# Four reorderings in a fused attention and feed-forward block: sums, norms, a copy and three tiles' products change places

## The chip, the cores and the metric

The kernel runs on one core of a Trainium2 chip. A core has a matmul engine (TensorE, PE in the profile; PEld is its weight load), a vector engine (VectorE, DVE), an activation engine (ScalarE, ACT), a general engine (GpSimd, POOL) and SyncE (SP), which here only issues DMAs. Each engine takes its own instructions in the order in which the program wrote them, and waits on semaphores for the others. The metric is the time of one execution on the device in microseconds (us); lower is better.

## The reference

Eight sequences of 1024 rows and 256 columns pass through an attention without learned projections and then through a feed-forward block. Both are wrapped in a layer norm whose scale, shift and gate come from a small vector per sequence:

```python
h = _layernorm(x, axis=-1) * (1 + ca) + sa
x = x + ga * _L0_attn_ref(h, L0_attn_w_lhs, L0_attn_w_rhs)
h = _layernorm(x, axis=-1) * (1 + cb) + sb
x = x + gb * _L0_ffn_ref(h, L0_ffn_W1, L0_ffn_b1, L0_ffn_W2, L0_ffn_b2)
```

The attention is `softmax((h * w_lhs) @ (h * w_rhs).T) @ h`, and the feed-forward block is `relu(h @ W1 + b1) @ W2 + b2` with 1024 inner columns. All is float32.

## The kernel before

**Tiles and stages.** A sequence is a "batch" b (0 to 7) of eight row tiles i of 128 rows; a half g is four of them. The main loop runs over (b, i). In iteration (b, i) the kernel works on several things at once: it makes the scores of the tile two ahead (`direct`, L410, copied out of PSUM by ACT, L417), mirrors them into the rows below, since scores of a symmetric kind are computed once (`mirror`: a DVE transpose L433, four DMA writes and one read through DRAM by SP), takes the row maximum of that tile (`row_max`, L460), turns the maximum into a row with a PE transpose (`max_turn`, L465), subtracts it (`subtract`, L472) and takes the exponential (`exponent`, L481); multiplies the weights with the values (`product`, L493, or the pair functions at L544 and L584 that save products by sums); and does one piece of the feed-forward of the batch before. The tiles with i % 4 below 2 are called "first" in the code and carry the feed-forward's first layer; the other two carry its second layer (`y_first`, `y_second`, L798).

**Order.** The order of the instructions is written out by hand. Each call in the loop emits its instructions to the queues of its engines at that point, and a pinning step keeps that order on each engine. So to move a call is to move its instructions on each engine that it uses, and on no other. Small sums for POOL are kept in a list (`later`), of which `spare()` emits one at a time.

**The first layer.** It is done in chunks c of pairs of inner column blocks. `pair_products(b, g, c)` emits the products pa, pb and pc (L718) and an ACT copy of pa, called kept (L739). `pair_sums` emits four DVE sums (L754, L757, L760, L763) that read pb, pc and kept; when it is done the PSUM banks of pb and pc are free again. `pair_last` emits one more product into pa, a DVE sum (L771) and a POOL sum (L772). `pair_relu` emits two ACT relus (L781, L782) on the tile f, and `pair_turn` four POOL sums (L791 to L794). In the last batch pb lies in another group of PSUM banks.

**Norms.** `ffn_rstd` emits two ACT operations, a logarithm and an exponential (L245, L246), that make one over the root of a variance; the variance is made by `pair_stats` (DVE, L239 and L240). `ffn_norm` makes the normalised rows X, in batch 0, half 0, with four DVE operations (L655), elsewhere with ACT (L650). In iteration (0, 6) `norms` calls just that `ffn_norm(0, 0)`; `ffn_blocks(0, 0)` returns at once. In (0, 7), `ffn_turn(0, 0)` transposes these rows on PE (L687) and shifts and scales them into hT on DVE and ACT (L697, L699); POOL then makes the sums hs (L706 to L709).

**The last phase.** After the loop the feed-forward of the last batch is done with W2 multiplied by the gate (w2g). For each half g it does four chunks of the first layer, and then `second(b, a, parts, cut)` for the four tiles a: eight products (L903) over the inner column blocks, in the order 0, 4, 1, 5, 2, 6, 3, 7. Part 0 is the first `cut` of them (here six), part 1 the rest; the last two need the relu of the last chunk. `second_out` adds the rows x on DVE (L917) and has SP write them out (L919, L921), tiles in pairs, but for the last two.

Of the kernel before, what the change touches and what calls it, by code (L numbers as in the profile page):

```python
# [24 lines left out]
def adaln_block_kernel(  # L25
# [14 lines left out]
    B, S, D = x.shape  # L40
# [3 lines left out]
    NI = INTER // P  # L44
    HALF = 512
    TH = HALF // P
# [411 lines left out]
    def row_max(b, i):  # L458
        m = work.tile([P, 1], F32, tag="m", name=f"m_{b}_{i}")
        nc.vector.tensor_reduce(m, score_row(b, i), AX.XY, ALU.max)  # L460
        max_t[b, i] = m
# [167 lines left out]
    def spare():  # L629
        if queue:  # L630
            queue.popleft()()
# [4 lines left out]
    def ffn_rstd(b, g):  # L636
        mv = mvb_t.pop((b, g))
        ffn["r", g] = mv, rstd_of(mv, "rb", f"rb_{b}_{g}")
# [140 lines left out]
    def pair_relu(c):  # L779
        f = ffn["f"]  # L780
        nc.scalar.activation(f[:, c, :], f[:, c, :], AF.Relu)  # L781
        nc.scalar.activation(f[:, c + NH, :], f[:, c + NH, :], AF.Relu)  # L782
# [325 lines left out]
    def norms(b, i):  # L1108
        if b > 0 and i == 0:
            ffn_blocks(b - 1, 1)  # L1110
        if b == 0:
            if i == 0:
                prepare_start(1)
                prepare_stats(1, 0)
            elif i == 1:
                prepare_stats(1, 1)
                sum_w1()
        elif b + 1 < B:
            if i == 1:
                prepare_start(b + 1)  # L1120
                prepare_stats(b + 1, 0)
            elif i == 2:
                prepare_blocks(b + 1, 0)
                x_plus(b + 1, 0)
                xg_times(b + 1, 0)
        elif i == 4:

            ffn_blocks(b, 0)
        if b == B - 1:
            return  # L1130
        if i == 6:
            if b == 0:
                ffn_norm(b, 0)
            ffn_blocks(b, 0)
# [7 lines left out]
    for b in range(B):  # L1142
        for i in range(NT):
# [8 lines left out]
            if (b, i) == (0, NT - 2):  # L1152

                prepare_turn(1, 1)
                product(b, i)
                direct(*ahead)
                exponent(*last_exponent)
                product_out(b, i)
                mirror(*ahead)
                early(b, i)  # L1160
                for _ in range(4):
                    spare()
                row_max(*ahead)
                late, last_exponent = ahead, None
                norms(b, i)
                continue
            if ahead and ahead != (0, 2):
                direct(*ahead)
# [34 lines left out]
            if first:  # L1203

                ub, ug = (b - 1, 0) if i >= TH else (b - 2, 1)
                back = i % TH == 0 and ub >= 0
                pair_products(fb, fg, c, turn_max)
                if i == 0:
                    ffn_rstd(b - 1, 1)
                if (b, i) == (1, 0):  # L1210
                    weights(*late)
                    late = None
                if i == TH + 1:
                    pair_relu(c - 1)
                pair_sums(fb, fg, c)
                if ahead:
                    mirror(*ahead)
                pair_last(fb, fg, c)
                if (b, i) == (B - 1, TH):
                    pair_stats(b, 2)  # L1220
                    ffn_rstd(b, 0)
                if i == 0 and back:
                    for q in range(2):
                        y_add(ub, ug, q)
                if i == TH + 1:
                    pair_turn(c - 1)
                if i == 4 and b + 1 < B:
                    prepare_blocks(b + 1, 1)
                    xg_times(b + 1, 1)
                if late:  # L1230
                    subtract(*late)
                pair_products(fb, fg, c + 1, (lambda: max_turn(*extra)) if extra else None)
                if i == 5:
                    exponent(*late)
                    if b + 1 < B:
                        prepare_turn_apart(b + 1, 1, 1)
                        prepare_turn_apart(b + 1, 1, 0)
                pair_relu(c)
                sides_too = i == 4 and b + 1 < B
                if sides_too:  # L1240
                    prepare_turn_apart(b + 1, 0, 1)
                if late and i != 5:
                    exponent(*late)
                if sides_too:
                    prepare_turn_apart(b + 1, 0, 0)
                middle(b, i)
                pair_sums(fb, fg, c + 1)
                pair_last(fb, fg, c + 1)
                if ahead and ahead != extra:
                    row_max(*ahead)  # L1250
                pair_turn(c)
                if i == 0:
                    right_sums(b, (3,))
                    pair_relu(c + 1)
                    pair_turn(c + 1)
                elif back:
                    for q in range(2):
                        y_add(ub, ug, q)
                if c > 0:
                    pair_relu(c + 1)  # L1260
                    pair_turn(c + 1)
            else:
                half = i % TH - 2
                if i == 3 and b + 1 < B:
                    prepare_stats(b + 1, 1)
                if half == 0:
                    if i == 2:
                        pair_begin(b, i, turn_max)
                    else:
                        pair_begin(b, i, lambda: (max_turn(*late), weights(*late)))  # L1270
                elif not ahead:

                    pair_end(b, i - 1)
                    pair_out(b, i - 1)
                    pair_stats(b, i - 1)
                if half:
                    y_second(fb, fg, turn_max)
                else:
                    y_first(fb, fg)
                if i == NT - 2 and (b, 2) in two_t:  # L1280
                    pair_stats(b, 2)
                if ahead:
                    mirror(*ahead)
                if i == 2 and b + 1 < B:
                    prepare_rstd(b + 1, 0)
                elif i == 3 and b + 1 < B:
                    prepare_rstd(b + 1, 1)
                elif i == 6 and b + 1 < B:
                    ffn_rstd(b, 0)
                elif i == NT - 1 and b == B - 1:  # L1290
                    ffn_rstd(b, 1)
                if half == 0:
                    pair_begin_sum(b, i)
                    if i == 2:
                        weights(*late)
                    left_sums(b, i)
                spare()
                early(b, i)
                if late and half:
                    weights(*late)  # L1300
                middle(b, i)
                if i == 2 and b + 1 < B:
                    load_x(b + 1, 1)
                if i == 3 and b + 1 < B:
                    prepare_norm(b + 1, 1)
                    x_plus(b + 1, 1)
                spare()
                if ahead:
                    row_max(*ahead)
                if half:  # L1310
                    y_second_sums(fb)
                else:
                    y_first_sums()
                spare()
# [32 lines left out]
    b = B - 1  # L1347
    for g in range(NT // TH):
        for c in range(NH):
            pair_products(b, g, c)  # L1350
            if g == 0 and c == 0:
                ffn_norm(b, 1)
                ffn_bias(b, 1)
            spare()
            spare()
            if c > 1:
                pair_relu(c - 2)
            if c > 0:
                pair_last(b, g, c - 1)
            pair_sums(b, g, c)  # L1360
            if g == 0 and c == 1:
                ffn_blocks(b, 1)
            elif g == 0 and c == 2:
                y_turn(b - 1, 1)
        pair_relu(NH - 2)
        pair_last(b, g, NH - 1)
        pair_relu(NH - 1)
        if g == 0:
            y_add(b - 1, 1, 0)
            y_add(b - 1, 1, 1)  # L1370
            y_out(b - 1, 1)
            ffn_turn(b, 1)
        for a in range(g * TH, (g + 1) * TH, 2):

            second(b, a, (0,), NI - 2)
            second(b, a + 1, (0,), NI - 2)
            second(b, a, (1,), NI - 2)
            second_out(b, a)
            second(b, a + 1, (1,), NI - 2)
            second_out(b, a + 1)  # L1380
            for _ in range(4):
                spare()
    pin(pin_from)


# [37 lines left out]
```

## Time and profile before

| | |
|---|---|
| Runs (three) | 769.8, 769.78 and 769.23 us; median 769.78 us |
| The profiled execution | 769.46 us, of which the span of the profile is 767.7 us |
| PE busy | 756.5 us, 99% of the span, 3708 matmuls |
| DVE busy | 566.0 us, 74% |
| POOL busy | 538.9 us, 70% |
| ACT busy | 375.0 us, 49% |
| DMA | 95.18 MB moved, mean 124 GB/s |
| TensorE clock granted | 0.9 or more in each of 40 slices |

How to read it: a busy share is an average over all stages. PE's end times are modelled and neighbouring matmuls overlap in the record, so the start of the next matmul tells more than the end of the last one. "Idle before, releaser" names the instruction that ended an engine's idle time. Idle time of an engine other than the one that sets the pace costs nothing by itself. The span runs from the first to the last instruction of the program; the execution's time includes 1.76 us around it.

### The profile page before, as it was taken

The numbers are of one execution on the slowest core, as the hardware profiler recorded it, in microseconds if no ns is written. First come the engines' busy times: TensorE is split into PE (matmuls) and PEld (weight loads), VectorE is DVE, ScalarE is ACT, GpSimd is POOL, SyncE is SP. The second block draws the span as 40 slices with busy tenths as digits, with TensorE's granted clock in tenths as the row PEclk, the third lists the DMA queues.
The fourth block names the chain that finished last, engine by engine and source line by source line (L and its number), as shares of the span: only waits on it lengthen the run. The fifth ranks groups of instructions, "written<-read, shape, count | busy, mean of one in ns | idle before, by whom it ended". The sixth has DMA issues, their size and how long they took to land.

```text
span 767.7 us, 11489 instructions
## 1 busy us (share of the span) xinstructions
PE 756.5 (99%) x3708; PEld 621.7 (81%) x3708; DVE 566.0 (74%) x1222; ACT 375.0 (49%) x681; POOL 538.9 (70%) x632
## 2 busy tenths in 40 slices
PE   8999999999999999999999999999999999999998
PEld 3576789888887888878888888988888788879886
DVE  6697779678796787858787787966879677594632
ACT  4464545635465355555546444563546535252511
POOL 4643975978859697587868787597884979469641
PEclk9999999999999999999999999999999999999999
DMA  5314434365343553535443554436534354142220
GB/s 194 124 50 137 116 104 109 112 192 168 93 131 107 183 150 111 151 102 160 139 124 122 151 151 131 107 117 189 163 98 131 104 159 139 33 134 80 82 83 27
DMA packets 106211, 95.18 MB, mean 124 GB/s; under 512 B 29700, under 2 KB 98848, under 8 KB 106152
## 3 DMA queue, kind: packets, MB, share of 16 engines
q1 hardware_dynamic: 98408, 85.81, 38.1%
q10 hardware_dynamic: 7744, 8.65, 3.7%
q8 instruction: 29, 0.48, 0.2%
q14 instruction: 30, 0.25, 0.1%
HBM read 50.62 MB, written 43.81 MB: 123 GB/s over the span
## 4 chain that ended last, share of the span: by engine, by line
PE 93%; DVE 3%; POOL 1%; issue 1%; ACT 1%; DMA 1%; SPq 0%; DVEq 0%; POOLq 0%
PE po L493 16%; PE psc L410 15%; PE pa L718 10%; PE pb L718 7%; PE pc L718 7%; PE yc L798 6%; PE ya L798 6%; PE yb L798 6%; PE pr L584 5%; PE pq L584 3%; PE pp L544 3%; PE py L903 3%; PE yd L798 3%; PE pm L465 1%; POOL xg L285 1%
## 5 line engine op out<-in xcount | busy, mean ns | idle before, releaser
L772 POOL TENSOR_TENSOR f<-f,kept 128x512 f32<-128x512 f32 x64 | 81.5, 1273 | 105.6 <-DVE f L771 100.2
L410 PE MATMUL psc<-rT,lT 128*128 128x512 f32 (+3 forms) x384 | 134.6, 486 | 0.0
L493 PE MATMUL po<-xg,pT 128*128 128x257 f32 x576 | 131.6, 380 | 0.0
L493 PEld LDWEIGHTS po<-xg,pT 128*128 128x128 f32 x576 | 108.8, 190 | 16.0 <-issue 1.0
L472 DVE TENSOR_TENSOR pT<-sc,pm 128x1024 f32<-128x1024 f32 x64 | 77.1, 1205 | 29.0 <-PE pm L465 24.9
L410 PEld LDWEIGHTS psc<-rT,lT 128*128 128x128 f32 x384 | 67.6, 190 | 38.0 <-issue 26.3
L417 ACT COPY sc<-psc 128x512 f32<-128x512 f32 (+3 forms) x96 | 44.9, 476 | 108.3 <-PE psc L410 94.7
L481 ACT ACTIVATE pT<-pT 128x1024 f32<-128x1024 f32 x64 | 67.4, 1052 | 34.6 <-DVE pT L472 34.6
L460 DVE TENSOR_REDUCE m<-sc 128x1 f32<-128x1024 f32 x64 | 77.3, 1208 | 0.0
L739 ACT COPY kept<-pa 128x512 f32<-128x512 f32 x64 | 37.3, 583 | 79.6 <-PE pa L718 79.6
L718 PE MATMUL pb<-hs,w1s 128*128 128x256 f32 x256 | 65.8, 379 | 1.0 <-DVE f L757 1.0
L718 PE MATMUL pc<-hT,w 128*128 128x256 f32 x256 | 65.7, 379 | 0.0
L781 ACT ACTIVATE f<-f 128x512 f32<-128x512 f32 x64 | 40.1, 626 | 48.6 <-POOL f L772 48.4
L634 POOL TENSOR_TENSOR x<-x,rows 128x256 f32<-128x256 f32 x64 | 45.3, 741 | 22.3 <-DVE x L509 11.8
L718 PEld LDWEIGHTS pb<-hs,w1s 128*128 128x128 f32 x256 | 48.0, 190 | 8.5 <-DVE f L757 1.4
L718 PEld LDWEIGHTS pc<-hT,w 128*128 128x128 f32 x256 | 48.6, 190 | 6.6
L798 PE MATMUL yc<-f,w2s 128*128 128x256 f32 x224 | 52.1, 379 | 0.0
L798 PEld LDWEIGHTS yc<-f,w2s 128*128 128x128 f32 x224 | 41.5, 190 | 10.1 <-issue 2.9
L433 DVE STREAM_TRANSPOSE Tm<-sc 128x896 f32<-128x896 f32 (+6 forms) x49 | 34.7, 707 | 13.3 <-ACT sc L417 12.6
L793 POOL TENSOR_TENSOR ft<-ft,f 128x256 f32<-128x256 f32 x56 | 40.8, 728 | 4.4
L792 POOL TENSOR_TENSOR ft<-ft,f 128x256 f32<-128x256 f32 x56 | 40.8, 728 | 4.4
L791 POOL TENSOR_TENSOR ft<-f 128x256 f32<-128x256 f32 x56 | 40.9, 731 | 3.4 <-ACT f L782 3.4
(165 smaller groups left out, 1670.2 us busy)
## 6 DMA issues: line engine op xcount, KB each, us to landing
D_f<-T_f SPq DMA_DIRECT2D x60, 128.0 KB, 2.7
X_f<-D_f SPq DMA_DIRECT2D x15, 512.0 KB, 3.8
D_a<-T_a SPq DMA_DIRECT2D x56, 128.0 KB, 3.2
D_y<-T_y SPq DMA_DIRECT2D x56, 128.0 KB, 3.0
Y<-D_y SPq DMA_DIRECT2D x14, 512.0 KB, 3.3
out_dram<-x SPq DMA_DIRECT2D x14, 512.0 KB, 3.9
X_a<-D_a SPq DMA_DIRECT2D x13, 512.0 KB, 3.6
x<-in_L_attn_x_dram ACTq DMA_DIRECT2D x12, 512.0 KB, 4.1
```

The costliest lines, as they stand in the source:

```text
L410: nc.tensor.matmul(psc[:, : hi - lo], lhsT=lT_t[b, i // TH][:, k, ts(i % TH, P)], rhs=rT_t[b, n][:, k, lo - n * HALF : HALF], start=(k == ...
L417: nc.scalar.copy(score_row(b, i)[:, lo // V : hi // V, :], psc[:, : hi - lo].rearrange("p (n v) -> p n v", v=V),)
L460: nc.vector.tensor_reduce(m, score_row(b, i), AX.XY, ALU.max)
L472: nc.vector.tensor_tensor(pT.rearrange("p j (a v) -> p j a v", v=V), score_columns(b, i), pm[:, :P].rearrange("p (j a v) -> p j a v", j=1, ...
L481: nc.scalar.activation(pT_t[b, i], pT_t[b, i], AF.Exp)
L493: nc.tensor.matmul(po[:, : D + 1], lhsT=pT[:, t, :], rhs=xg_t[b][:, t, 0 : D + 1], start=(t == 0), stop=(t == NT - 1),)
L584: nc.tensor.matmul(out, lhsT=lhs[:, t, :], rhs=rhs[:, t, :], start=(t == 0), stop=(t == TH - 1),)
L634: queue.append(lambda: nc.gpsimd.tensor_tensor(out, in0, row, op))
L718: nc.tensor.matmul(out, lhsT=lhsT, rhs=rhs, start=True, stop=True)
L772: nc.gpsimd.tensor_tensor(f[:, c::NH, hi], f[:, c::NH, hi], kept[:, None, hi].to_broadcast([P, 2, H2]), ALU.add,)
L791: add(ft[:, 0, c], f[:, c + NH, hi], f[:, c, hi], ALU.subtract)
L798: nc.tensor.matmul(out, lhsT=lhs(c), rhs=rhs(c), start=(c == 0), stop=(c == NH - 1))
```

## The change

Four calls, or groups of calls, change places; nothing is added or taken away.

1. In iteration (0, 6) `norms(b, i)` (four DVE operations) is emitted before `row_max(*ahead)` (one), not after it.
2. In iteration (1, 0) `weights(*late)`, which is the subtraction on DVE and the exponential on ACT for tile (1, 0), is emitted after `pair_sums` of the first chunk and not before it. The lines with `TH + 1` move in the text only; they belong to other iterations.
3. In iteration (7, 4) `ffn_rstd(b, 0)` is emitted after the products of the second chunk, and so after that chunk's copy kept on ACT.
4. In the last phase the first six products of three tiles of a half are emitted one tile after another. Then the last two products and the output of each of the three follow, and then all eight products and the output of the fourth tile. Before, two tiles' first parts came together, then their last parts, and then the next two tiles.

```diff
@@ -1160,9 +1160,9 @@
                 early(b, i)
                 for _ in range(4):
                     spare()
+                norms(b, i)
                 row_max(*ahead)
                 late, last_exponent = ahead, None
-                norms(b, i)
                 continue
@@ -1207,18 +1207,17 @@
                 pair_products(fb, fg, c, turn_max)
                 if i == 0:
                     ffn_rstd(b - 1, 1)
+                if i == TH + 1:
+                    pair_relu(c - 1)
+                pair_sums(fb, fg, c)
                 if (b, i) == (1, 0):
                     weights(*late)
                     late = None
-                if i == TH + 1:
-                    pair_relu(c - 1)
-                pair_sums(fb, fg, c)
                 if ahead:
                     mirror(*ahead)
                 pair_last(fb, fg, c)
                 if (b, i) == (B - 1, TH):
                     pair_stats(b, 2)
-                    ffn_rstd(b, 0)
@@ -1230,6 +1229,8 @@
                 if late:
                     subtract(*late)
                 pair_products(fb, fg, c + 1, (lambda: max_turn(*extra)) if extra else None)
+                if (b, i) == (B - 1, TH):
+                    ffn_rstd(b, 0)
                 if i == 5:
@@ -1370,16 +1371,15 @@
-        for a in range(g * TH, (g + 1) * TH, 2):
-
+        tiles = range(g * TH, (g + 1) * TH)
+
+        for a in tiles[:3]:
             second(b, a, (0,), NI - 2)
-            second(b, a + 1, (0,), NI - 2)
-            second(b, a, (1,), NI - 2)
+        for a in tiles:
+            second(b, a, (0, 1) if a == tiles[3] else (1,), NI - 2)
             second_out(b, a)
-            second(b, a + 1, (1,), NI - 2)
-            second_out(b, a + 1)
-            for _ in range(4):
-                spare()
+            spare()
+            spare()
```

Names used below: TH is 4 (tiles in a half), NI is 8 (inner column blocks), B is 8.

## The prediction

> **What bounds the kernel now.** I read the page first, then the waits of TensorE (PE) alone, then the timeline around each wait and around the end. All times are in microseconds (us) from the start of the span.
>
> ```profile
> PE 93%; DVE 3%; POOL 1%; issue 1%; ACT 1%; DMA 1%; SPq 0%; DVEq 0%; POOLq 0%
> ```
>
> This is the head of the chain that ended last: 93% of it is matmuls. PE is the bound, and a change pays only where PE stands still. The waits of PE, with total, number and longest, name four places that the change touches:
>
> ```profile
> PE pa L718 <- ACT kept L739: 1.4, 1, 1.4
> PE py L903 <- ACT f L781: 1.1, 2, 0.7
> PE pb L718 <- DVE f L757: 1.0, 1, 1.0
> ...
> PE ptx L687 <- DVE X_f L655: 0.2, 1, 0.2
> ```
>
> Modelled ends blur these figures, so I measure each wait by start to start. The timeline (start, length, engine, line, operation, tiles, count, and the idle time before it) shows where they stand, first on PE:
>
> ```profile
> 71.24 1.74 PE L687 MATMUL ptx<-ident,X_f 128*128 128x128 f32 x8 [0.24 <-DVE X_f L655]
> ...
> 82.43 0.59 PE L718 MATMUL pa<-hs,w 128*128 128x256 f32 x2
> 84.02 1.13 PE L718 MATMUL pb<-hs,w1s 128*128 128x256 f32 x4 [1.00 <-DVE f L757]
> ...
> 677.98 0.70 PE L718 MATMUL pa<-hT,w1s 128*128 128x256 f32 x2 [1.36 <-ACT kept L739]
> ...
> 702.64 1.95 PE L584 MATMUL pq<-tsum,pT 128*128 128x129 f32 x16
> ...
> 722.59 1.89 PE L903 MATMUL py<-w2g,f 128*128 128x256 f32 x8
> 725.17 12.50 PE L903 MATMUL py<-w2g,f 128*128 128x256 f32 x56 [0.69 <-ACT f L781]
> ```
>
> and then what stands in front of it on the other engines:
>
> ```profile
> 69.68 1.18 DVE L460 TENSOR_REDUCE m<-sc 128x1 f32<-128x1024 f32 x1
> 70.78 1.37 DVE L655 TENSOR_SCALAR X_f<-x,mvb,rb 128x256 f32<-128x256 f32 x4
> ...
> 81.76 1.22 DVE L472 TENSOR_TENSOR pT<-sc,pm 128x1024 f32<-128x1024 f32 x1 [2.74 <-PE pm L465]
> ...
> 676.92 0.30 ACT L245 ACTIVATE rb<-mvb,eps 128x4 f32<-128x4 f32 x1 [4.48 <-DVE mvb L240]
> ...
> 700.97 1.27 POOL L566 TENSOR_TENSOR pT<-s,pT 128x512 f32<-128x512 f32 x1
> ```
>
> A maximum stands before the norms at 69.68, a subtraction before the sums at 81.76, a root before a copy (677.36 to 677.93) at 676.92; and in the last phase PE stops after 8 matmuls, which are four products, as each product of 256 columns is issued as two.
>
> **What the Trainium skill says.** "Perfetto Trace Analysis", section "Tensor Engine Instruction (MATMUL, LD_WEIGHTS)", has ACT, DVE and GpSimd as strict FIFO and the matmul end as estimated. The trace agrees: the copy at 677.36 has its input from the matmul that starts at 674.30, and still follows the root. "SBUF — State Buffer", section "SBUF: two separate sides", names a port lock between a DVE operation with two SBUF inputs and a GpSimd operation. All sums and subtractions moved here read one operand from PSUM, so I charge nothing; the trace has POOL's L529 at 1.27 beside the subtraction's 1.22, both as elsewhere. "DMA: Bandwidth & Descriptors", section "Anatomy of one DMA — SWDGE (gpsimd) path", puts most of a fixed 2 us of a transfer into the write receipt. Here the last 128 KB write, issued by SP's queue, lands 1.7 after its issue; I use that.
>
> **Part A: norms before the maximum, iteration (0,6).** Nothing is added. The four norms (L655, 1.37) change places with one row maximum (1.18 of L460, 1.10 start to start). The norms start at 69.68 and end at 71.05, and the maximum ends at the old 72.15. The last score matmul starts at 70.41 and keeps PE for 0.43, so PE could transpose from 70.84. In place of eight transposes paced by the norms, it does eight at 0.107, ending at 71.70 instead of 72.81: -1.11. The maximum is read by the transpose at 81.45 and has nine microseconds of slack. The mirror transpose (72.07) and hT (72.96) come after both and do not move. So POOL's row hs, w2s, tsum, which starts at 73.81 and runs without a gap to 85.66, doesn't move either; hs ends at 76.70, and PE reads it at 78.86 - 1.11 = 77.75.
>
> **Part B: sums before the subtraction, iteration (1,0).** The matmul pb of the second pair waits for a PSUM bank that L757 of the first pair frees at 83.97, because L754 and L757 stand behind the subtraction (1.22). Unstalled, pb would start at 82.86 and its second matmul at 83.07 instead of 84.34: 1.26. With A, the first pair's pb ends at 79.64. Then L754 starts at 79.74, L757 at 80.26, L760 at 80.66, L763 ends at 81.47, and the subtraction runs from 81.39 to 82.60. Behind the subtraction on DVE stand the mirror of row 2 and L771, all still earlier than before. Behind it through the data stands the exponential on ACT (82.64 to 83.69), and behind that on ACT the copy kept of the second pair, to 84.17. This is the wait that replaces the old one: PE reaches the last product of the second pair at 85.96 - 1.11 - 1.26 = 83.59 and starts it at 84.22. Measured starts after a stall (84.02, then 84.34) cost a further 0.10. The gain after that is 1.64 and not 2.37.
>
> A second limit follows. POOL is busy to 85.66, so L772 gains only 0.27, and with it on ACT the relus, the norms L650, the exponential and the copy at 93.09, all in a row: that copy now ends near 93.2. PE would read it at 94.73 - 1.64 = 93.09. About 0.2 goes with restart: A and B together give 1.45. Bounds: 1.2 if POOL and ACT run a little later, 1.7 if the copy is in time. DVE and POOL catch up at their next idle times (1.83 at 99.92 and 0.80 at 105.76), and from there on everything hangs on PE, batch after batch (143.93, 235.04, 326.15 for the same row, 91.11 apart), so the gain should last.
>
> **Part C: the copy before the root, iteration (7,4).** The copy's input ends near 674.9, the root's at 676.89. With the copy first, PE goes on at 676.46 instead of 677.98, with 0.10 of restart less: -1.6 at that place. But DVE's row does not move: it is without idle time from 670.07 to 681.17. So L771 ends at 680.05 as before, and POOL starts L772 at 680.19, and from there POOL has no gap until L567 ends at 703.65. At the end of that row PE needs L566 (ends 702.24) for pq at 702.64: slack 0.40. PE arrives 1.5 early, waits for L564, L565 and L566 in turn, and starts pq at 702.30 with a restart of 0.10. Kept: 0.24. Bounds: 0 if the restarts cost more, 1.6 if POOL's row shifts after all. The root itself still waits for L240 at 676.89, so nothing behind it on ACT is later. L320 may come 0.5 earlier, without a reader in need.
>
> **Part D: three tiles' early products first, last batch.** Per half the same 32 products run, the first six of the first tile in the old order. PE waits at the fifth product, for the relu that ends at 725.12, and this wait stays: 0.86 start to start here, 0.59 in the second half (751.92). What the change covers better is the relu of the last pair; it ends at 727.60, and PE came to it after 12 products, at 725.17 + 8 x 0.43 = 728.6, so it waited for nothing. Gain 0. The adds L917 of the first tiles and the write of tiles 4 and 5 come some 2.4 later (757.95 to about 760.3), tile 6 earlier, tile 7 not at all, and tile 7's write at 764.86, landed at 766.57, sets the end. POOL's list of spare work is empty by then (last L634 at 718.05). SP's order of writes is unchanged. Bounds: -0.2 to +0.2.
>
> **The sum.** 1.45 + 0.24 + 0 = 1.69. The profiled execution took 769.46, with 1.76 around its span of 767.7; less 1.69 that is 767.77. It lies 0.32 under the median of the runs shown, 769.78, from which the sum gives 768.09. I forecast 767.9, between the two. A measurement of this kernel can tell about 0.2% (1.54) from no change, and the forecast lies close to that line.
>
> **Rivals.**
> 1. *More is given back* (17%): POOL's fixed row in batch 1 holds PE longer than 0.2, as L772 (85.89, 0.23 after L529) and the relus behind it hardly move. For: POOL idles only 0.23, 0.77 and 0.40 up to 96.82. Against: 1.83 at 99.92. With 0.8 from A and B and 0.2 from C: 768.6.
> 2. *C keeps its full wait* (13%): POOL's row is not the limit, for example because the norms' earlier end pulls it forward. For: 1.36 is the largest single wait. Against: POOL shows no idle from 680.19 on. 1.45 + 1.5 = 2.95: 766.7.
> 3. *The waits only change their names* (5%): the reordering doesn't reach what it aims at, as I expect of D, and A and B are lost in batch 1 too: 769.6.
> 4. *Slower* (7%): the place is the ACT queue in (1,0). The subtraction now waits for all four sums, and each microsecond that it comes later delays the exponential, the copy behind it and PE's last product. The old start of that product, 85.96, is reached if the subtraction starts at 83.1; with C's 0.24 counted, the kernel is slower by 1.5 if it starts past 84.9, and then stands at 771.2. That takes a sum held by 3.5 more than computed, which no row shows.
>
> **How the numbers follow.** The main case has 58%, from 767.2 to 768.5. Range: from 766.5 (rival 2) to 769.0 (most of rival 1); left out are slower, unchanged and a few per cent at the ends. Faster by over 0.2% means below 768.24: four fifths of the main case and all of rival 2, 60%. Slower by over 0.2% is rival 4, 7%. The rest, 33%, lies within 0.2%.
>
> **What would show it.** A: the transposes ptx start at 0.11 apart near 70.85, with po near 71.7. B: no wait of pb for L757, a short new one for kept L739 near 84, another near 93. C: no wait near 678, three short waits of PE for POOL near 698 to 701 in L584. D: the two waits of py for L781 remain. The prediction fails if PE waits at other places in batches 1 to 6, if pq has no wait at all, or if py's waits shrink.

## The result and the profile after

| | before | after |
|---|---|---|
| Median of 19 runs each | 769.73 us | 768.27 us |
| Range of these runs | 769.23 to 771.0 us | 767.67 to 769.02 us |
| Ratio of after to before, 95% interval | | 0.998 (0.9973 to 0.9987) |
| Span of the profiled execution | 767.7 us | 766.5 us |

The kernel became 1.46 us (0.19%) faster at the median, and the interval leaves out no change. The median lies 0.37 us over the forecast of 767.9. It also lies 0.03 us over 768.24, the prediction's line for "faster by over 0.2%", and so in the band to which it gave 33% and not in the one to which it gave 60%.

The head of the chain that ended last, on the page of the kernel after:

```profile
PE 95%; DVE 2%; POOL 1%; DMA 1%; issue 1%; ACT 1%; SPq 0%; POOLq 0%; DVEq 0%
```

and the waits of PE in it (total, times, longest, in us):

```profile
PE py L903 <- ACT f L781: 1.1, 2, 0.7
...
PE pa L718 <- ACT kept L739: 0.5, 1, 0.5
...
PE pq L584 <- POOL pT L566: 0.3, 1, 0.3
PE pr L584 <- POOL pT L565: 0.2, 1, 0.2
```

Three old waits are gone from this list: ptx for DVE, pb for L757, and the 1.4 of pa for kept in the last batch. In their places stand three new, shorter ones, and py's wait stands there untouched. (A fourth that is new, 0.6 of pth at 10.59, belongs to the start of the program, which differs from run to run.) The timeline of PE after, at these places:

```profile
71.18 1.04 PE L687 MATMUL ptx<-ident,X_f 128*128 128x128 f32 x8
...
82.10 1.03 PE L718 MATMUL pb<-hs,w1s 128*128 128x256 f32 x4
...
84.64 0.70 PE L718 MATMUL pa<-hT,w1s 128*128 128x256 f32 x2 [0.54 <-ACT kept L739]
...
675.40 0.59 PE L718 MATMUL pa<-hT,w1s 128*128 128x256 f32 x2
...
698.58 1.16 PE L584 MATMUL pr<-tsum,s 128*128 128x128 f32 x8
699.93 1.16 PE L584 MATMUL pr<-tsum,pT 128*128 128x128 f32 x8 [0.19 <-POOL pT L565]
701.34 2.05 PE L584 MATMUL pq<-tsum,pT 128*128 128x129 f32 x16 [0.25 <-POOL pT L566]
...
721.39 1.89 PE L903 MATMUL py<-w2g,f 128*128 128x256 f32 x8
723.97 12.50 PE L903 MATMUL py<-w2g,f 128*128 128x256 f32 x56 [0.69 <-ACT f L781]
```

The eight transposes now take 1.04 and not 1.74. pb follows its predecessor without a wait, and 2.5 us later pa waits for the copy. In the last batch pa starts with no wait at 675.40, and PE then stands three times in L584: 0.25, 0.46 and 0.52 by the starts against before, of which the view marks only the last two.

To follow a gain through the program, I take the start of the same matmul in two traces; a negative shift means earlier. The first 70 us differ from run to run (the last score matmul ahead of the transposes ptx lay between 0.15 us earlier and 0.51 later than before in the traces of this study), so each row is counted from that matmul. Here po is the product of the attention in that iteration, and "after pb" and "behind pq" mean from the second matmul of each on:

| Start of PE's work, against before | at po (0,7) | after pb (1,0) | at po (1,0) | in (1,1) to (7,4) | at po (7,4) | behind pq (7,7) | at the end |
|---|---|---|---|---|---|---|---|
| after | -1.10 | -2.37 | -1.57 | -1.41 | -3.03 | -1.55 | -1.54 |

That one row is the whole story: 2.37 is gained, 0.80 and then 0.16 are given back; 1.62 is gained, 1.48 is given back; the last phase adds nothing.

### The profile page after: what moved, and what is told of

Read it like the earlier page. It is cut to its first block, busy times and chain, and to the rows that moved or that the text cites. A ratio compares the mean times of both kernels' runs of the same rounds, so it can differ in the third digit from the quotient of the medians.

```text
span 766.5 us, 11489 instructions
## 1 busy us (share of the span) xinstructions
PE 756.5 (99%) x3708; PEld 621.8 (81%) x3708; DVE 566.4 (74%) x1222; ACT 374.9 (49%) x681; POOL 539.3 (70%) x632
## 4 chain that ended last, share of the span: by engine, by line
PE 95%; DVE 2%; POOL 1%; DMA 1%; issue 1%; ACT 1%; SPq 0%; POOLq 0%; DVEq 0%
PE po L493 16%; PE psc L410 16%; PE pa L718 10%; PE pb L718 7%; PE pc L718 7%; PE yc L798 6%; PE ya L798 6%; PE yb L798 6%; PE pr L584 5%; PE pq L584 3%; PE pp L544 3%; PE py L903 3%; PE yd L798 3%; PE pm L465 1%; POOL xg L285 1%; DMA x<-in_L_attn_x_dram 1%
## 5 line engine op out<-in xcount | busy, mean ns | idle before, releaser
L772 POOL TENSOR_TENSOR f<-f,kept 128x512 f32<-128x512 f32 x64 | 81.5, 1275 | 101.9 <-DVE f L771 96.8
L718 PE MATMUL pb<-hs,w1s 128*128 128x256 f32 x256 | 65.8, 379 | 0.0
L718 PE MATMUL pc<-hT,w 128*128 128x256 f32 x256 | 65.7, 379 | 0.0
L781 ACT ACTIVATE f<-f 128x512 f32<-128x512 f32 x64 | 40.1, 626 | 50.2 <-POOL f L772 50.1
L634 POOL TENSOR_TENSOR x<-x,rows 128x256 f32<-128x256 f32 x64 | 45.4, 743 | 22.3 <-DVE x L509 11.8
L718 PEld LDWEIGHTS pb<-hs,w1s 128*128 128x128 f32 x256 | 48.1, 190 | 7.5 <-DVE f L757 0.4
L718 PEld LDWEIGHTS pc<-hT,w 128*128 128x128 f32 x256 | 48.6, 190 | 6.6
L798 PE MATMUL yc<-f,w2s 128*128 128x256 f32 x224 | 52.1, 379 | 0.0
L798 PEld LDWEIGHTS yc<-f,w2s 128*128 128x128 f32 x224 | 41.5, 190 | 10.1 <-issue 2.9
L791 POOL TENSOR_TENSOR ft<-f 128x256 f32<-128x256 f32 x56 | 41.0, 732 | 4.5 <-ACT f L782 4.4
L792 POOL TENSOR_TENSOR ft<-ft,f 128x256 f32<-128x256 f32 x56 | 40.8, 729 | 4.4
```

Of the source, the lines that this page charges most:

```text
L634: queue.append(lambda: nc.gpsimd.tensor_tensor(out, in0, row, op))
L718: nc.tensor.matmul(out, lhsT=lhsT, rhs=rhs, start=True, stop=True)
L772: nc.gpsimd.tensor_tensor(f[:, c::NH, hi], f[:, c::NH, hi], kept[:, None, hi].to_broadcast([P, 2, H2]), ALU.add,)
L791: add(ft[:, 0, c], f[:, c + NH, hi], f[:, c, hi], ALU.subtract)
L798: nc.tensor.matmul(out, lhsT=lhs(c), rhs=rhs(c), start=(c == 0), stop=(c == NH - 1))
```

## The experiments

The ratios are to runs of the kernel before that were taken beside each group, with medians of 769.63 to 769.66 us. "Shift" is the start of PE's last work against before, counted as above, from one trace of each kernel.

| Run | Median us | Ratio to before (95%) | Shift |
|---|---|---|---|
| e1_norms: A alone | 768.53 | 0.9985 (0.9979 to 0.9992) | -1.10 |
| e2_sums: B alone | 769.13 | 0.9993 (0.9985 to 1.0001) | -0.47 |
| e3_root: C alone | 769.57 | 0.9998 (0.999 to 1.0006) | -0.20 |
| e4_tiles: D alone | 769.62 | 1.0001 (0.9993 to 1.0009) | -0.01 |
| e5_exp: after, later exponential | 767.94 | 0.9977 (0.9968 to 0.9986) | -1.55 |
| e6_tsum: that, tsum moved | 767.54 | 0.9971 (0.9959 to 0.9983) | -2.20 |
| e7_yadd: after, y_add on DVE | 767.06 | 0.9965 (0.9953 to 0.9978) | -2.55 |
| e8_cut: after, cut of four | 766.14 | 0.9952 (0.994 to 0.9965) | -3.51 |
| e10_cutpair: before, cut of four | 768.43 | 0.9987 (0.998 to 0.9993) | -1.31 |
| e9_all: after, all of these | 764.88 | 0.9939 (0.9927 to 0.9952) | -5.07 |

### The four parts, each alone

A alone (e1_norms):

```diff
+                norms(b, i)
                 row_max(*ahead)
                 late, last_exponent = ahead, None
-                norms(b, i)
```

> Part A alone on the kernel before (norms ahead of the maximum in iteration (0,6)). Theory: the eight transposes ptx run 0.11 us apart, po starts 1.1 us sooner after the last score matmul, and all of it lasts to the end, because the limits behind it (the kept copy of (1,1) near 93.2) leave 1.5 us of room: -1.1 us, ratio 0.9986. Rival (POOL's fixed row in batch 1 gives more back): the trace shows a new wait of PE between 73 and 105, and at most -0.6 us is left.

Measured: 768.53 us, shift -1.10 at po, and -1.10 to -1.11 at every place behind it. PE's timeline in this run:

```profile
70.69 1.04 PE L687 MATMUL ptx<-ident,X_f 128*128 128x128 f32 x8
71.56 3.63 PE L493 MATMUL po<-xg,pT 128*128 128x257 f32 x16
```

From the first transpose to po it is 0.87 us, where the working had 0.86 (eight times 0.107). The rival that POOL's row takes part of A alone falls.

B alone (e2_sums):

```diff
+                pair_sums(fb, fg, c)
                 if (b, i) == (1, 0):
                     weights(*late)
                     late = None
-                pair_sums(fb, fg, c)
```

> Part B alone on the kernel before (four sums ahead of the subtraction in (1,0)). Theory: the wait of pb for L757 (1.26 us start to start) goes, the copy kept of the second pair stands behind a later exponential and holds PE's last product of that pair for about 0.6 us: -0.55 us is left, ratio 0.9993. Rival 1 (the exponential is no limit): -1.26 us and no wait for kept. Rival 2 (the later subtraction costs more than the wait): no change or slower.

Measured: 769.13 us. The shift is -1.27 behind pb and -0.47 behind the new wait, which is this one (in order of time: the exponential on ACT, the copy behind it, and PE, which waits for the copy):

```profile
83.96 1.06 ACT L481 ACTIVATE pT<-pT 128x1024 f32<-128x1024 f32 x1 [2.87 <-DVE pT L472]
...
84.92 0.57 ACT L739 COPY kept<-pa 128x512 f32<-128x512 f32 x1
...
85.54 0.70 PE L718 MATMUL pa<-hT,w1s 128*128 128x256 f32 x2 [0.54 <-ACT kept L739]
```

The copy's input is ready at 83.2 (the end of the matmul that starts at 82.57), and the copy runs at 84.92, behind the exponential. So 0.80 of the 1.27 is a wait with a new name. Both rivals fall by the trace; the interval of the times alone still holds no change.

C alone (e3_root):

```diff
                     pair_stats(b, 2)
-                    ffn_rstd(b, 0)
...
                 pair_products(fb, fg, c + 1, (lambda: max_turn(*extra)) if extra else None)
+                if (b, i) == (B - 1, TH):
+                    ffn_rstd(b, 0)
```

> Part C alone on the kernel before (copy ahead of the root in (7,4)). Theory: PE starts the product behind the copy 1.5 us sooner, and then waits two or three times for POOL's sums L564 to L566 in (7,7): -0.15 to -0.25 us is left, ratio 0.9997. Rival (POOL's row moves with PE): -1.5 us, no wait in L584.

Measured: 769.57 us; the interval of the times alone can't tell it from no change. The trace can: the shift is -1.64 at po of (7,4), -1.37 a few microseconds on, and -0.19 behind pq, where PE stands just as in the kernel after:

```profile
699.89 1.16 PE L584 MATMUL pr<-tsum,s 128*128 128x128 f32 x8
701.24 1.16 PE L584 MATMUL pr<-tsum,pT 128*128 128x128 f32 x8 [0.19 <-POOL pT L565]
702.65 2.05 PE L584 MATMUL pq<-tsum,pT 128*128 128x129 f32 x16 [0.25 <-POOL pT L566]
```

pq starts at 702.65, where it was at 702.64 before. As this trace started 0.30 late, 0.30 of the 1.64 us is left at pq's first matmul, and 0.19 from its second on.

D alone (e4_tiles) is the last hunk of the change on the kernel before:

```diff
+        for a in tiles[:3]:
             second(b, a, (0,), NI - 2)
...
+        for a in tiles:
+            second(b, a, (0, 1) if a == tiles[3] else (1,), NI - 2)
             second_out(b, a)
```

> Part D alone on the kernel before (three tiles' first six products ahead). Theory: the two waits of py for L781 stay (0.69 and 0.43 by the list of waits), the end is set by tile 7 as before: 0 us, ratio 1.0000, at most 0.2 either way. Rival: the waits shrink, -0.5 us or more; or the later write of tiles 4 and 5 sets the end, +0.5 us.

Measured: 769.62 us, shift -0.01. The list of PE's waits has the same line for py and L781 as before (1.1 in two waits, the longest 0.7). The span is 767.8 us against 767.7, with a start that was 0.16 late, so the later write doesn't set the end either.

The four shifts add up to -1.78; together the kernel has -1.54. Of the missing 0.24, 0.16 is A and B, which are worth 1.57 by their sum and 1.41 together: a second limit, next. Most of the rest is C, which keeps 0.20 alone and 0.14 here.

### Where the gain of B went: two limits in a row

The run e5_exp takes the new wait of B away. The exponential is emitted behind the second pair's products, and so behind their copy on ACT:

```diff
                 if (b, i) == (1, 0):
-                    weights(*late)
-                    late = None
+                    subtract(*late)
...
-                if late:
+                if late and (b, i) != (1, 0):
                     subtract(*late)
                 pair_products(fb, fg, c + 1, (lambda: max_turn(*extra)) if extra else None)
...
+                if (b, i) == (1, 0):
+                    exponent(*late)
+                    late = None
```

> The changed kernel, with the exponential of (1,0) emitted after the second pair's products, so that the copy kept of that pair is ahead of it on ACT. Theory (two limits in a row in batch 1: first this copy, then the copy of (1,1) that hangs on POOL's fixed row): the wait of 0.54 us for kept L739 near 84.6 goes, and comes back near 93.5; 0 to -0.1 us against the changed kernel. Rival (the copy is the only limit): -0.6 us against it, no wait for kept.

Measured: shift -2.37 at po of (1,0), in place of -1.57, and -1.41 in (1,1), the same as without the edit. PE's timeline has no wait at 83.75, where it was taken away, and a larger one in its stead at 93.38:

```profile
83.75 0.60 PE L718 MATMUL pa<-hT,w1s 128*128 128x256 f32 x2
...
93.38 0.70 PE L718 MATMUL pa<-hT,w1s 128*128 128x256 f32 x2 [0.70 <-ACT kept L739]
```

The median is 0.33 us under the changed kernel's, more than expected, but the intervals overlap and the trace has 0.01, so no gain is shown. The later copy stands at the end of a row on ACT that begins with a relu, and that relu waits for POOL (ACT's timeline in this run):

```profile
87.12 0.63 ACT L781 ACTIVATE f<-f 128x512 f32<-128x512 f32 x1 [3.19 <-POOL f L772]
...
92.75 0.58 ACT L739 COPY kept<-pa 128x512 f32<-128x512 f32 x1
```

The run e6_tsum therefore adds to it a change on POOL: batch 1's four sums tsum (`right_sums`, L529) go to iteration (1,2). Three of them stood ahead of that L772, the fourth behind it, at 91.58 in the changed kernel:

```diff
                     assert not queue
-                    right_sums(1, range(3))
...
-                    right_sums(b, (3,))
+                    if b > 1:
+                        right_sums(b, (3,))
...
+                    if (b, i) == (1, 2):
+                        right_sums(b, range(4))
                     left_sums(b, i)
```

> As the run before, and batch 1's four sums tsum (L529) on POOL are moved from the front of L772 to the front of left_sums in (1,2). Theory: L772 starts some 1.7 us sooner, the relus, norms and copies on ACT follow, both waits for kept are gone, and -0.7 us is kept against the changed kernel. Rival (another limit stands behind, or the moved sums make PE wait in (1,3)): 0, or slower, with a wait of PE in L584 near 117.

Measured: 767.54 us, shift -2.20. POOL's timeline has L772 behind DVE's sums and no longer behind tsum (86.00 in the changed kernel). The view names L647, which comes on DVE right behind the sum L771 that L772 needs:

```profile
84.11 1.27 POOL L772 TENSOR_TENSOR f<-f,kept 128x512 f32<-128x512 f32 x1 [2.04 <-DVE rs_f L647]
```

and PE's timeline has no wait left in (1,1):

```profile
92.58 0.60 PE L718 MATMUL pa<-hT,w1s 128*128 128x256 f32 x2
93.01 0.59 PE L718 MATMUL pa<-hT,w 128*128 128x256 f32 x2
```

The whole 2.37 now stands in (1,1). A new wait of pb for L757 at 126.17 takes 0.34 of it. By the timeline DVE is late there through one operation ahead of its transposes of Y: its last L612 (123.25) takes 0.69, where it takes 0.34 in the changed kernel. Beside it runs POOL's L634, which now stands behind the moved sums and ends at 123.80; in the changed kernel it ends at 122.06, before that L612 begins. e9_all has the same pair. That the moved sums cause this was not tried by itself.

### Where the gain of C went: POOL's row

In the changed kernel pq starts at 701.34, just after this sum of POOL ends at 701.28:

```profile
699.95 1.33 POOL L566 TENSOR_TENSOR pT<-s,pT 128x512 f32<-128x512 f32 x1
```

The run e7_yadd takes 2.5 us out of POOL's row in the last batch. The two sums y_add, which add the result Y of the feed-forward to the rows x, go to DVE, behind the maximum of (7,5), and pair_turn of chunk 1 goes ahead of L772:

```diff
-        nc.gpsimd.tensor_tensor(x2, x2, y, ALU.add)
+        engine.tensor_tensor(x2, x2, y, ALU.add)
...
+                if (b, i) == (B - 1, TH + 1):
+                    pair_turn(c - 1)
                 pair_last(fb, fg, c)
...
-                elif back:
+                elif back and b < B - 1:
                     for q in range(2):
                         y_add(ub, ug, q)
+                elif (b, i) == (B - 1, TH):
+                    read_back()
+                elif (b, i) == (B - 1, TH + 1):
+                    for q in range(2):
+                        y_add(b - 1, 0, q, nc.vector)
+                    y_out(b - 1, 0)
```

> The changed kernel, with the two sums y_add (L868, 2.5 us of POOL) of (7,4) done by DVE at the end of (7,5), and pair_turn of chunk 1 ahead of L772 of chunk 2 on POOL. Theory (POOL's row from 680 to 704 takes back part C): the waits of PE for L564 to L566 go and the whole of C is kept, -1.1 us against the changed kernel. Rival (DVE's row is the limit as well, or something else waits in (7,7)): less than -0.4 us, or slower if DVE's added 1.3 us reaches PE.

Measured: 767.06 us, 1.21 under the changed kernel; shift -2.55, 1.01 further. PE in (7,7) has no wait any more:

```profile
698.16 1.05 PE L584 MATMUL pr<-tsum,s 128*128 128x128 f32 x8
699.05 1.06 PE L584 MATMUL pr<-tsum,pT 128*128 128x128 f32 x8
699.95 1.95 PE L584 MATMUL pq<-tsum,pT 128*128 128x129 f32 x16
```

So it was POOL's row, and not DVE's, that took C back; which of the two edits to that row was needed was not tried. Of the 1.62 us, 1.12 now lasts to the end (-2.55 against -1.43 ahead of C). The rest goes in two small steps before L584: 0.25 at the pb that waits for L757 (683.39), as in the changed kernel, and 0.24 at ya (L798, 694.63). The second is a price of the edit, by the timeline: ya starts just after ACT's copy L810 ends (694.49), that copy stands behind an exponential, and the exponential waited 2.92 us for a DVE subtraction that now comes after the two y_add.

### Why part D does nothing: the cut

e8_cut lets the first part of the three tiles be four products long and not six:

```diff
         for a in tiles[:3]:
-            second(b, a, (0,), NI - 2)
+            second(b, a, (0,), NI - 4)
         for a in tiles:
-            second(b, a, (0, 1) if a == tiles[3] else (1,), NI - 2)
+            second(b, a, (0, 1) if a == tiles[3] else (1,), NI - 4)
```

> The changed kernel, with a first part of four products and not six (NI - 4) for the first three tiles of a half. Theory (part D does nothing because the fifth product of the first tile still waits for the relu of the chunk before the last): twelve products stand ahead of that relu's rows, both waits of py for L781 go, -1.7 us against the changed kernel. Rival (the relus are late for another reason, or the output at the end sets the time): -0.3 us or less.

Measured: 766.14 us, 2.13 under the changed kernel; shift -3.51, of which 1.90 is gained in this phase. PE does the 64 matmuls of each half in one go, the first of them here:

```profile
721.07 13.98 PE L903 MATMUL py<-w2g,f 128*128 128x256 f32 x64
```

Is it the cut or the third tile? e10_cutpair has only the cut, with the tiles in pairs as before:

```diff
-            second(b, a, (0,), NI - 2)
-            second(b, a + 1, (0,), NI - 2)
...
+            second(b, a, (0,), NI - 4)
+            second(b, a + 1, (0,), NI - 4)
+            second(b, a, (1,), NI - 4)
...
+            second(b, a + 1, (1,), NI - 4)
```

> The kernel before, with tiles in pairs as they were, and only the first part cut to four products (NI - 4). Theory (the cut is what matters, and three tiles instead of two add the rest): eight products cover the relu of the chunk before the last, but not all of the last one's; one or two short waits of py for L781 or L782 remain, -1.3 to -1.6 us against the kernel before, some 0.5 less than the same cut gave with three tiles. Rival (three tiles are what matters): -0.5 us or less.

Measured: 768.43 us, shift -1.31. The 64 matmuls take 14.41 in the first half and 14.14 in the second, and not 13.98. Over both halves the weight load still waits 0.7 in two times for L781 and 0.2 for L782; in the first half PE stands at 727.00, at the first product that needs the last chunk. So the cut alone brings 1.3, and the third tile brings the rest of 1.9, but only with that cut.

### All together

> The changed kernel with all the edits tried on it together: the later exponential, the moved tsum sums, y_add on DVE with pair_turn ahead, and the cut of four. Theory (the limits lie in separate stages and add up): -0.7, -1.1 and -2.0 us, 764.3 us in all, ratio 0.9931, and no wait of PE over 0.3 us is left after 72 us. Rival (they overlap, since each sets the same engines back): 765.3 us or more.

Measured: 764.88 us, ratio 0.9939 (0.9927 to 0.9952), shift -5.07. Adding the shifts of the single runs to the changed kernel's 1.54 (0.66, 1.01 and 1.97) gives 5.18, so the limits lie in separate stages; the median, between theory and rival, is 0.6 us over the first and hides this in part, since the start of the program varies by as much. The waits of PE in this run:

```profile
PE pw L141 <- DVE early_a L129: 1.5, 1, 1.5
PE pmc L208 <- ACT cols L177: 0.8, 2, 0.5
PE ptm L449 <- ACT sc L450: 0.7, 1, 0.7
PE pth L358 <- POOL xg L285: 0.5, 1, 0.5
PE pm L465 <- DVE rl L507: 0.4, 1, 0.4
```

None of the changed kernel's new waits in the stages of the four parts is in the list any more; the five that are left lie in the first 48 us and stood in both kernels' lists. This kernel is faster than both: its ratio and interval are against the kernel before, and against the changed one its median is 3.39 us less.

## Why the prediction was right, point by point

- **A, -1.11 predicted.** -1.10 in the changed kernel and -1.10 alone. The order of norms and maximum was the cause, and nothing behind it takes it back.
- **B, 1.26 for the wait of pb, then 0.73 given back.** Measured 1.27 and 0.80; the 0.07 between is L757, which started 0.59 after L754 (80.10, then 80.69) where the working had 0.52, and everything behind it followed. The new wait stands where the prediction put it: pa of the second pair, for the copy kept behind the exponential (predicted start 84.22; measured 84.64, or 84.29 with the later start of that trace taken off). e2_sums shows it alone, and e5_exp shows that it goes with the exponential.
- **The second limit in (1,1), about 0.2.** Measured 0.16. That it hangs on POOL's row was only argued then; e5_exp and e6_tsum show it. "A and B together give 1.45": measured 1.41. That it lasts, batch after batch: the shift is -1.41 in (1,2), (1,4) and at the head of (7,4).
- **C, 1.6 at the place and 0.24 kept.** Measured 1.62 and 0.14 in the changed kernel, 0.20 alone. The three waits of PE in L584 are the ones named. The term that was too large is the slack of pq: POOL's L566 took 1.33 in this trace and not 1.27, and L564 came 0.03 later than the rest of the shift. In each of the twelve traces the one sum of this row that takes 1.33 is the one that starts while DVE's L697 runs. Before, that was L567 (702.32), on which pq does not wait. L697 comes earlier with PE (699.30 to 700.16 in this trace), POOL's row does not, and so it falls on L566. No run moved L697 alone. A wait of pb for L757, 0.25 of the shift between po of (7,4) and the middle of (7,5), was not foreseen; it lies inside the time that PE then waits for POOL, so it costs nothing here.
- **D, nothing.** -0.01, for the reason given: the fifth product of the first tile still waits. The working also said that the last pair's relu needs no more cover than twelve products give. That holds only while the first wait stands: in e10_cutpair, where it is gone, PE comes to that relu after ten products and waits. The gain of the right cut is also larger than the two waits, 0.86 and 0.59 start to start, since the starts behind each wait are too far apart as well.
- **The sum, -1.69.** The trace has -1.54; the medians have -1.46. So 0.23 of the 0.37 us to the forecast is gain that was missing, 0.15 of it in the trace. The other 0.14 is the starting point: 767.9 and 1.69 make 769.59, between the profiled execution and a median of three runs, and the later median of 19 lies at 769.73.
- **The rivals.** More given back: A and B kept 1.41 and not 0.8. C in full: no, POOL's row was the limit. Waits that only change their names: true of part of B and nearly all of C. Slower by the later subtraction: it starts at 81.81, or 81.46 with the later start of the trace taken off, where the working had 81.39 and the gain of B would be lost only at 83.1.

## What to carry to other kernels

When one engine is busy 99% of the time, list its own waits and cost each by the start of the next instruction; then ask what the next engine in line can deliver at the earlier time. An engine whose row of work has no gap (here POOL from 680 to 704) takes back what a gain ahead of it has over its slack, here all but 0.14 to 0.20 of 1.62 us, and work had to be moved off that row before the gain was real. Where products are ordered to cover a late input, count from the first product that needs a late input and not from the last: one number, the cut of four, brought 1.97 us on top of the changed kernel, more than the four reorderings together (1.54), though only 1.31 on the kernel before, without the third tile.

## What the runs showed of the hardware

**DVE and POOL in turn.** Where a DVE sum had both inputs in SBUF, it and POOL's sums took turns. In e7_yadd the two y_add run on DVE (128x512 each) among POOL's sums:

```profile
688.53 2.05 DVE L868 TENSOR_TENSOR x<-x,Y 128x512 f32<-128x512 f32 x2
...
687.63 1.27 POOL L772 TENSOR_TENSOR f<-f,kept 128x512 f32<-128x512 f32 x1 [0.51 <-DVE f L771]
688.86 1.18 POOL L791 TENSOR_TENSOR ft<-f 128x256 f32<-128x256 f32 x1
690.11 1.06 POOL L792 TENSOR_TENSOR ft<-ft,f 128x256 f32<-128x256 f32 x1
```

The two y_add take 0.92 and 1.21 and end at 689.45 and 690.58; POOL's three sums end at 688.90, 690.04 and 691.17. So the ends alternate, each 0.54 to 0.59 after one of the other engine, and L791 and L792 take 1.18 and 1.06 in place of 0.73. The Trainium skill says so on its page "SBUF — State Buffer", section "SBUF: two separate sides": a DVE operation with two SBUF inputs and a GpSimd operation that reads SBUF exclude one another. The alternating ends agree; the page has no figure for such sums. DVE's sums and subtraction with one operand in PSUM, moved in part B, left POOL's tsum at 1.27 to 1.29 in the changed kernel. The L612 of e6_tsum that took 0.69 also reads both its tensors from SBUF; it ends 0.14 after POOL's L634.

DVE's L697, which reads one tensor from SBUF and writes to SBUF, shows the same. In the kernel before it takes 0.55 at 166.26, with no POOL work beside it, and 1.57 at 113.04, beside L567 (113.06 to 114.33). There, and in (7,7) in all twelve traces, it ends 0.28 or 0.29 after the POOL sum. The prediction did not look at this pair.

**After a stall.** At three stalls of L718, PE lost 0.10 us more than the wait itself: matmuls that start 0.22 apart elsewhere start 0.32 apart there (84.64 and 84.96 in the kernel after, and the same at 84.02 and at 677.98 in the kernel before). At the two stalls of py (725.17 and 751.92 before) some of the next starts were 0.29 or 0.30 apart as well, and 0.25 and 0.19 were lost beyond the wait. With 0.86 and 0.59 that makes 1.89, and e8_cut won back 1.90.
